# A top-1 expert layer: the routing of its first half issued in pieces between the blocks of its shared expert

## The chip, the core and the metric

The kernel runs on one core of a Trainium2 chip. A core has five engines, each with its own instruction queue, which it works through in order: TensorE (PE, matrix products and transposes; its weight loads are a row of their own, PEld), VectorE (DVE, elementwise work and reductions), ScalarE (ACT, activation functions and copies), GpSimd (POOL, elementwise work and the issue of indirect DMAs) and SyncE (SP, the issue of plain DMAs). They wait for each other through semaphores. The metric is the device time of one execution in microseconds; a median over several runs is given.

## What is computed

A decoder of four layers; each has a self attention, a cross attention and a feed-forward part, all with a residual. x is 32 x 128 tokens of 128 floats. The change lies in the feed-forward part of layer 2, a top-1 mixture of seven experts with a shared eighth one that every token passes. Cut to what matters:

```python
def _L2_ffn_ref(x, Wr, Wu, Wg, Wd, Wu_s, Wg_s, Wd_s):
    def _swiglu(x, wu, wg, wd):
        up = x @ wu
        g = x @ wg
        gate = jax.nn.sigmoid(g) * g
        return up * gate @ wd
    logits = x @ Wr
    probs = jax.nn.softmax(logits, axis=-1)
    topk_vals, topk_idx = jax.lax.top_k(probs, TOP_K)
    out = jnp.zeros_like(x)
    for i in range(TOP_K - 1):
        p = topk_vals[..., i:i + 1]
        ind = topk_idx[..., i]
        acc = jnp.zeros_like(x)
        for j in range(NUM_EXPERTS - 1):
            mask = (ind == j).astype(x.dtype)[..., None]
            acc = acc + _swiglu(x, Wu[j], Wg[j], Wd[j]) * mask
        out = out + ALPHA * p * acc
    out = out + _swiglu(x, Wu_s, Wg_s, Wd_s)
    return out

x = x + _L2_ffn_ref(_layernorm(x, axis=-1), L2_ffn_Wr, ...)
```

With TOP_K 2 the loop runs once, so each token goes to its best expert, unless that is number 7, which has no expert. DIM is 128, HID 512.

## The kernel before

x stays on the chip in eight groups `xg[0]` to `xg[7]` of 512 tokens (4 tiles of 128). Most tiles come from pools with a fixed number of slots that are reused in turn: `bmid` (5 slots of 128x512), `gmid` (10), `bbig` (4 of 128x2048), the small `s` tiles, and in PSUM `ps`, `two` and `acc` (two slots each). A tile whose slots are all in use waits for the release of one. A scheduler orders each engine's instructions by the order of the program and by when it reckons them ready. Between `follow(T, A, V)` (L243) and `follow()` the engines named keep the order of the program; POOL and SP are never held to it. In this layer `follow` isn't used before the change; in the attention ahead of it and in the layer behind it is.

The layer is `layer8` (L1509), called once for each half of the tokens (side 0 is groups 0 to 3, side 1 groups 4 to 7), and driven by `layer8_first` (L1783):

1. `ready(i)` normalizes group i into `xn_all` (`norm`, L336: bn_stats and bn_aggr on DVE, an addition and a power on POOL, the scaling of four tiles on DVE). `gate(i)` turns it over on PE, copies it on ACT to `xnTs[i]`, a `gmid` tile, and takes the logits into one `acc` tile.
2. `route()` (L1551): softmax over 8 logits of 16 tiles at once, one Exp on ACT and the rest on DVE. `first_k` (L418) ranks by comparing all pairs, on two `bbig` tiles of 128x1024. It leaves the selection `ssel` and the weight of the expert `ww2`.
3. `place()` (L1566): two products with triangular and full matrices of ones, a scan and small DVE operations give each token its row `pos` in a buffer `xs` in DRAM sorted by expert, and each tile of sorted rows the row `wrow` of its expert's weights. POOL clears one of the scratch tiles (`keep8`, L1574).
4. `ready2(i)` normalizes half two. `send(c)` (16 times, L1606) stores a tile of 128 normalized tokens to `xs` by an indirect DMA from POOL. `load(t)` (L1633) fetches the weights of sorted tile t, 768 KB, into one of four `units` slots, also an indirect DMA from POOL. `rows(t)` (L1639) reads sorted rows, a plain DMA on SP, which waits for all stores, and copies their row numbers on POOL.
5. `shared(i, c)` (L1612): one of 16 blocks of the shared expert, group i and quarter c of the hidden width. Two up products into a `two` tile, Silu on ACT, product by gate on DVE, down product into an `acc` tile. Each 128x512 float32 product is two matmul passes in the trace. After the fourth quarter `add_out` (L409) copies the sum (ACT and DVE by turns, `evac`), turns it over and adds it to x. The shared weights `U[8]` hold one of the four `units` slots until the last block.
6. `gate2`, `route2`, then the experts of half one: `up(t)` and `down(t)` for 14 tiles of 256 rows, with further loads and rows, `place2` after tile 0, the stores of half two two by two, then `collect`. Half two's experts and its shared expert are handed to the next layer as work between its own steps.

Of the kernel before, what the change touches and what calls it, by code (L numbers as in the profile page):

```python
# [15 lines left out]
ALU = mybir.AluOpType  # L16
# [8 lines left out]
J = 4  # L25
# [177 lines left out]
def program(ctx, tc, cols, x, ctxt, mask, drop, dfirst, dsmall, dwide, drows, dunits, dexperts, dconst, drel, dwq, out):  # L203
# [32 lines left out]
    def bmid(shape=(128, 512)):  # L236
        return mid.tile(list(shape), F32, tag="bmid", name="bmid", bufs=5)

    def small(*shape):
        n = int(np.prod(shape))  # L240
        return sm.tile([128, *shape], F32, tag=f"s{n}", name="s", bufs=4 if n < 128 else 2)
# [12 lines left out]
    def flat(t):  # L254
        return t.rearrange("p a b -> p (a b)")

    def bc(ap, axis, n):

        ap = ap.unsqueeze(axis)
        shape = list(ap.shape)  # L260
        shape[axis] = n
        return ap.to_broadcast(shape)
# [73 lines left out]
    def norm(src, o, by=None, by2=None):  # L336

        st, mv, rs = small(J, 6), small(J, 2), small(J)
        for j in range(J):
            V.bn_stats(st[:, j, :], src[:, j, :])  # L340
        for j in range(J):
            V.bn_aggr(mv[:, j, :], st[:, j, :])
        if by is not None:
            P.tensor_tensor(rs, mv[:, :, 1], by2, ALU.mult)
            P.tensor_scalar(rs, rs, EPS, None, ALU.add)
        else:
            P.tensor_scalar(rs, mv[:, :, 1], EPS, None, ALU.add)
        P.tensor_tensor(rs, rs, K["nhalf"], ALU.pow)
        if by is not None:
            P.tensor_tensor(rs, rs, by, ALU.mult)  # L350
        for j in range(J):
            V.tensor_scalar(o[:, j, :], src[:, j, :], mv[:, j, 0:1], rs[:, j : j + 1], ALU.subtract, ALU.mult)
# [53 lines left out]
    def add_x(i, p):  # L406
        V.tensor_tensor(xg[i], xg[i], p, ALU.add)
# [7 lines left out]
            T.transpose(p[:, j, :], o[:, j * 128 : (j + 1) * 128], ident)  # L415
        add_x(i, p)

    def first_k(v, e, k, sel=None, n=J):  # L418

        tile_of = bmid if n * e * e <= 512 else bbig  # L420
        gt, eq = tile_of((128, n, e, e)), tile_of((128, n, e, e))
        other, own = bc(v, 2, e), bc(v, 3, e)
        V.tensor_tensor(gt, other, own, ALU.is_gt)
        V.tensor_tensor(eq, other, own, ALU.is_equal)
        tri = bc(K[f"tri{e}"], 1, n).rearrange("p a (i j) -> p a i j", i=e)
        V.tensor_tensor(eq, eq, tri, ALU.mult)
        V.tensor_tensor(gt, gt, eq, ALU.add)
        rank = small(n, e)
        sel = small(n, e) if sel is None else sel
        V.tensor_reduce(rank, gt, AX.X, ALU.add)  # L430
        V.tensor_scalar(sel, rank, k - 0.5, None, ALU.is_lt)
        return sel

    def parts3(w, parts):
# [1074 lines left out]
    def layer8(side):  # L1509
# [26 lines left out]
        ssel = sm.tile([128, N * J, 8], F32, tag="ssel", name="ssel", bufs=2)  # L1536
        ww2, pos = (sm.tile([128, N * J], dtype, tag=name, name=name, bufs=2) for name, dtype in (("ww2", F32), ("pos", I32)))
        wrow = sm.tile([128, TILES], I32, tag="wrow", name="wrow", bufs=2)
        xnTs, sums, ins, mids = {}, {}, {}, {}

        def ready(i):
            norm(xg[side * N + i], xn_all[:, i, :, 0:D])

        def gate(i):
            xnTs[i] = transposed(xn_all[:, i, :, 0:D], gmid(), A.copy)
# [5 lines left out]
        def route():  # L1551
            lg = sums.pop("l")
            l, m = bmid((128, N * J, 8)), small(N * J)
            V.tensor_reduce(m, lg, AX.X, ALU.max)
            V.tensor_tensor(l, lg, bc(m, 2, 8), ALU.subtract)
            A.activation(l, l, AF.Exp)
            V.tensor_reduce(m, l, AX.X, ALU.add)
            V.reciprocal(m, m)
            V.tensor_tensor(l, l, bc(m, 2, 8), ALU.mult)
            first_k(l, 8, 1, ssel, N * J)  # L1560
            V.tensor_scalar(l, l, 2.0, None, ALU.mult)
            V.tensor_tensor(l, ssel, l, ALU.mult)

            V.tensor_reduce(ww2, l[:, :, 0:7], AX.X, ALU.add)

        def place():  # L1566
            flat_sel = ssel.rearrange("p c e -> p (c e)")
            p = ps((128, 2, N * J * 8))
            mm(p[:, 0], K["upper"], flat_sel)
            mm(p[:, 1], K["ones"], flat_sel)  # L1570

            tot, ends, keep8 = (bmid((128, 8, N * J)) for _ in range(3))
            V.tensor_copy(tot, p[:, 1].rearrange("p (c e) -> p e c", e=8))
            P.memset(keep8, 1.0)  # L1574
            P.memset(keep8[:, :, 0:1], 0.0)
            V.tensor_tensor_scan(flat(ends), flat(keep8), flat(tot), 0.0, ALU.mult, ALU.add)
            rnd = 1.5 * 2.0**23

            nt, bt = small(8), small(8)
            V.tensor_scalar(nt, ends[:, :, N * J - 1], TOKENS / 2 - 0.5, 1.0 / TOKENS, ALU.add, ALU.mult)  # L1580
            V.tensor_scalar(nt, nt, rnd, rnd, ALU.add, ALU.subtract)
            below = small(8, 8)
            V.tensor_tensor(below, bc(nt, 1, 8), K["tri8"].rearrange("p (i j) -> p i j", i=8), ALU.mult)
            V.tensor_reduce(bt, below, AX.X, ALU.add)

            V.tensor_tensor(ends, ends, tot, ALU.subtract)
            first = small(8)
            V.tensor_scalar(first, bt, float(TOKENS), -1.0, ALU.mult, ALU.add)
            V.memset(first[:, 7:8], TILES * TOKENS - 1.0)
            V.tensor_tensor(ends, ends, bc(first, 2, N * J), ALU.add)  # L1590
            spot = bmid((128, N * J, 8))
            V.tensor_tensor(spot, p[:, 0].rearrange("p (c e) -> p c e", e=8), ends.rearrange("p e c -> p c e"), ALU.add)
            V.tensor_tensor(spot, spot, ssel, ALU.mult)
            posf = small(N * J)
            V.tensor_reduce(posf, spot, AX.X, ALU.add)
            V.tensor_copy(pos, posf)

            V.tensor_tensor(bt, bt, nt, ALU.add)
            past = bmid((128, TILES, 7))
            V.tensor_tensor(past, bc(K["count"][:, 0:TILES], 2, 7), bc(bt[:, 0:7], 1, TILES), ALU.is_ge)  # L1600
            ef = small(TILES)
            V.tensor_reduce(ef, past, AX.X, ALU.add)
            V.tensor_scalar(ef, ef, 6.0, 128.0, ALU.min, ALU.mult)
            V.tensor_tensor(wrow, ef, K["row"].to_broadcast([128, TILES]), ALU.add)

        def send(c):  # L1606
            at = bass.IndirectOffsetOnAxis(ap=pos[:, c : c + 1], axis=0)
# [1 line left out]
            tc.add_to_no_dep_group(f"rows{side}", d.ins)  # L1609
            tc.declare_no_dep(d.ins, group=f"rows{side}", reason="every token has a row of its own")  # L1610

        def shared(i, c):  # L1612
            if c == 0:
                sums[i] = acc()
            w8 = U[8]
            block = slice(c * 128, (c + 1) * 128)
            pa = two()
            mm(pa[:, 0], w8[:, 0:512][:, block], xnTs[i])
            mm(pa[:, 1], w8[:, 512:1024][:, block], xnTs[i])
            h = bmid()  # L1620
            A.activation(h, pa[:, 1], AF.Silu)
            V.tensor_tensor(h, h, pa[:, 0], ALU.mult)
            mm(sums[i], w8[:, 1024:1536][:, block], h, c == 0, c == 3)
            if c == 3:
                add_out(side * N + i, sums.pop(i))
                xnTs.pop(i)
                if i == N - 1:
                    U.pop(8)


        half = TOKENS // 128
# [143 lines left out]
            for i in range(N):  # L1775
                yield lambda: None, lambda i=i: collect(i)

        return ready, gate, route, place, send, shared, load, rows, up, down, collect, TILES, pieces


    beside = []
# [1 line left out]
    def layer8_first():  # L1783
        N = G // 2
        ready, gate, route, place, send, shared, load, rows, up, down, collect, TILES, _ = layer8(0)
        ready2, gate2, route2, place2, send2, _, load2, rows2, *_, pieces = layer8(1)
        for i in range(N):
            ready(i)
            gate(i)
        route()  # L1790
        place()
        for i in range(N):
            ready2(i)
        for c in range(N * J):
            send(c)
        load(0)
        load(1)
        load(2)
        rows(0)
        rows(1)  # L1800
        for i in range(N):
            for c in range(4):
                shared(i, c)
        for i in range(N):
            gate2(i)
        route2()
        later = [lambda c=c: send2(c) for c in range(N * J)]
        up(0)
        for t in range(TILES):
            if t + 3 < TILES:  # L1810
                load(t + 3)
            if t + 2 < TILES:
                rows(t + 2)
            if t + 1 < TILES:
                up(t + 1)
            down(t)
            if t == 0:
                place2()
            for _ in range(2 if t > 1 else 0):
                if later:  # L1820
                    later.pop(0)()
        for i in range(N):
            collect(i)

        def start():
            load2(0)
            load2(1)
            load2(2)
            rows2(0)
            rows2(1)  # L1830

        beside.append(start)
        beside.extend(pieces())
# [324 lines left out]
```

## Time and profile before

Most instructions carry the line of a helper (L192), so groups and stages are told apart by tiles and by time.

| | |
|---|---|
| runs shown, median (lowest to highest) | 2979.89 us (2970.95 to 2987.02) |
| profiled execution, its own time | 2967.81 us |
| its span, first to last instruction | 2965.9 us |
| PE, DVE, ACT, POOL busy | 86%, 70%, 51%, 33% |
| mean granted TensorE clock | 0.917 |
| chain that ended last, shares | PE 52%, DVE 29%, ACT 7%, POOL 7%, issue 3%, DMA 2% |

Busy shares are means over twelve parts with different limits; the layer of the change takes from about 2256 to 2447 us. A row of the timeline gives start, duration, engine, line, operation, the tiles written and read, and in brackets how long the engine had been idle and what released it. Durations are those of one execution.

The marks of the layer in the trace: the last matmul of half one's logits ends at 2267.8; `pos` and `wrow` are written at 2282.1 and 2282.2; the 16 stores are issued from 2282.6 to 2306.8; the shared expert's last down product ends at 2334.8; the logits of half two end at 2343.2; the experts' products run from 2343.5 to about 2435.8; half one's rows are collected at 2451.

### The profile page before, as it was taken

To read this page: it belongs to the slowest core of one execution; us is meant where nothing else is said; L and a number is where in the kernel's file an instruction comes from. 1 tells how busy PE (TensorE), PEld (TensorE's weight loads), DVE (VectorE), ACT (ScalarE), POOL (GpSimd) and SP (SyncE) were. 2 spreads that over 40 slices of the span, in tenths; PEclk is the share of its full clock that TensorE was granted. 3 is DMA by queue.
4 is the path that set the end of the run, shared out by engine and by line. 5 is a ranking of instruction groups with operands and counts; after the bars stand their busy time and mean duration, and the time that the engine had idled before them with its cause. 6 is when DMAs were issued, how large, how long until landed. Compare 5 with 4: busy or idle time off the path is not lost.

```text
span 2965.9 us, 55573 instructions
## 1 busy us (share of the span) xinstructions
PE 2552.0 (86%) x22609; PEld 1641.3 (55%) x22628; DVE 2072.2 (70%) x4121; ACT 1504.4 (51%) x3360; POOL 972.2 (33%) x1009
## 2 busy tenths in 40 slices
PE   6889999999889989999998999987886977976664
PEld 3555667777644446566664444445554666644443
DVE  6877667878878756677786544458886415789893
ACT  4555545444412256666664444457773323456663
POOL 4443342223210123334551000124442365324432
PEclk8877789999999999999999999989997998998786
DMA  3000000000000010000000000000002255210000
GB/s 113 2 2 2 6 20 8 5 8 1 12 11 1 0 33 2 5 9 9 12 2 15 1 1 0 1 1 2 2 2 82 94 179 166 91 29 12 22 11 18
DMA packets 50464, 73.44 MB, mean 25 GB/s; under 512 B 3841, under 2 KB 40962, under 8 KB 50082
## 3 DMA queue, kind: packets, MB, share of 16 engines
q1 hardware_dynamic: 41968, 33.05, 3.7%
q0 software_dynamic: 7808, 33.71, 3.5%
q8 instruction: 178, 2.92, 0.4%
q10 hardware_dynamic: 434, 3.14, 0.3%
q14 instruction: 76, 0.62, 0.1%
HBM read 57.00 MB, written 12.89 MB: 24 GB/s over the span
## 4 chain that ended last, share of the span: by engine, by line
PE 52%; DVE 29%; ACT 7%; POOL 7%; issue 3%; DMA 2%; DVEq 0%; ACTq 0%; POOLq 0%; SPq 0%
PE ps L192 21%; PE two L192 17%; PE acc L192 14%; DVE bbig L192 12%; DVE s L192 9%; DVE bmid L192 3%; DVE gmid L192 3%; ACT bbig L192 3%; POOL xn L399 3%; ACT bmid L192 1%; ACT xn L192 1%; POOL s L397 1%; DVE x L192 1%; ACT gmid L192 1%; DMA we<-in_experts,wrow 1%
## 5 line engine op out<-in xcount | busy, mean ns | idle before, releaser
L192 PE MATMUL ps<-cs,bbig 128*128 128x128 f32 x2208 | 330.3, 290 | 83.4 <-ACT bbig L192 34.6
L192 PEld LDWEIGHTS ps<-cs,bbig 128*128 128x128 f32 x2208 | 254.8, 147 | 187.3 <-ACT bbig L192 84.0
L192 ACT COPY bbig<-ps 128x512 f32<-128x512 f32 x418 | 229.2, 591 | 241.5 <-PE ps L192 241.4
L192 DVE TENSOR_REDUCE s<-two 128x8 f32<-128x1024 f32 (+1 forms) x192 | 234.1, 1220 | 119.6 <-PE two L192 118.4
L192 PE MATMUL two<-xnT,u 128*128 128x512 f32 x512 | 262.4, 613 | 11.8 <-ACT bmid L192 6.3
L192 DVE TENSOR_TENSOR bbig<-bbig 128x1024 f32<-128x1024 f32 (+3 forms) x234 | 249.6, 1108 | 7.3 <-ACT bbig L192 5.8
L192 PE MATMUL acc<-bmid,u 128*128 128x512 f32 x416 | 221.3, 619 | 20.1 <-DVE bmid L192 18.8
L192 PE MATMUL two<-gbig,gmid 32*128 32x512 f32 (+1 forms) x1248 | 216.5, 567 | 2.4 <-ACT bbig L192 2.4
L192 DVE TENSOR_TENSOR bmid<-bmid,ps 128x512 f32<-128x512 f32 x192 | 130.0, 684 | 114.8 <-ACT bmid L192 94.7
L479 POOL TENSOR_SCALAR gbig<-bmid,cs 128x512 f32<-128x512 f32 x96 | 148.7, 1565 | 162.8 <-ACT bmid L192 162.8
L192 ACT ACTIVATE bbig<-two,s 128x256 f32<-128x256 f32 (+1 forms) x512 | 189.7, 419 | 20.8 <-DVE s L192 17.4
L192 ACT ACTIVATE bbig<-bbig 128x512 f32<-128x512 f32 (+1 forms) x160 | 128.1, 801 | 87.1 <-DVE bbig L192 86.6
L192 PEld LDWEIGHTS two<-xnT,u 128*128 128x128 f32 x512 | 92.8, 193 | 116.4 <-issue 56.5
L192 ACT ACTIVATE bmid<-two 128x512 f32<-128x512 f32 x88 | 52.5, 597 | 183.3 <-PE two L192 175.0
L192 ACT ACTIVATE bmid<-two,ws 128x512 f32<-128x512 f32 x128 | 85.1, 686 | 115.1 <-PE two L192 115.0
L192 PEld LDWEIGHTS acc<-bmid,u 128*128 128x128 f32 x416 | 76.7, 197 | 115.1 <-DVE bmid L192 60.8
L192 ACT ACTIVATE bbig<-bbig,s 128x128 f32<-128x128 f32 x384 | 118.7, 388 | 29.0 <-DVE s L192 29.0
L1068 POOL TENSOR_TENSOR bbig<-bbig,s 128x1024 f32<-128x1024 f32 x32 | 60.6, 1893 | 214.2 <-PE two L192 152.7
L192 DVE TENSOR_TENSOR bbig<-two,s 128x1024 f32<-128x1024 f32 (+1 forms) x128 | 122.6, 958 | 9.0 <-ACT bbig L192 0.5
L491 POOL MEMSET val<- 128x512 f32 x72 | 39.5, 551 | 259.1 <-PE acc L192 258.1
L192 PE MATMUL ps<-cs,xn 128*128 128x128 f32 x288 | 66.5, 320 | 65.3 <-ACT xn L192 36.9
L192 PE MATMUL two<-xT,we 128*128 128x128 f32 (+1 forms) x576 | 102.5, 333 | 18.8 <-DMA we<-in_experts,wrow 14.8
(313 smaller groups left out, 5914.2 us busy)
## 6 DMA issues: line engine op xcount, KB each, us to landing
u<-in_units SPq DMA_DIRECT2D x10, 768.0 KB, 4.3
gmid<-in_ctx SPq DMA_DIRECT2D x16, 256.0 KB, 3.0
x<-in_x SPq DMA_DIRECT2D x8, 256.0 KB, 9.1
gmid<-in_mask SPq DMA_DIRECT2D x8, 256.0 KB, 3.1
ys<-bbig SPq DMA_DIRECT2D x2, 1024.0 KB, 6.6
gmid<-ys SPq DMA_DIRECT2D x8, 256.0 KB, 4.0
gmid<-in_drop SPq DMA_DIRECT2D x8, 256.0 KB, 3.4
out<-x SPq DMA_DIRECT2D x8, 256.0 KB, 2.4
```

The source lines that it names most:

```text
L192: d = f(*args, **kwargs)
L397: P.tensor_tensor(rs, rs, K["nhalf"], ALU.pow)
L399: P.tensor_scalar(xn[:, j, :], xg[i][:, j, :], mv[:, j, 0:1], rs[:, j : j + 1], ALU.subtract, ALU.mult)
L479: P.tensor_scalar(o[:, n, :], k, K["n4"][:, n : n + 1], None, ALU.mult)
L491: P.memset(o, 0.0)
L1068: (V if c2 else P).tensor_tensor(pr[:, four, :], pr[:, four, :], bc(nm[:, four], 2, 256), ALU.mult)
```

## The change

The routing functions become generators that give control back at marked places (`yield`), and the shared block is cut into four functions. After the logits of half one, all that follows runs as rounds under `follow(T, A, V)`: in round k the up products and Silu of block k, two pieces of routing, where it is due the turn-over and addition of the group that ended two rounds before, the down product of block k-1, and the gate product of block k. There are 21 pieces: the norm sums of half two (4), `route` (8), `place` (5), then, in one go with the first scaling of half two's norm, the three weight fetches, the 16 stores and the two row reads, and the other scalings. Thus the norm's sums and power are issued ahead of routing and its scalings behind the stores, and the fetches ahead of the stores. Scratch tiles of `place` come from `gmid` in place of `bmid`; the addition of EPS in half two's norm moves from POOL to DVE; the shared sums are all copied by ACT. Half two's `route2` and `place2` run the same pieces without a break between them.

```diff
+    def first_k_steps(v, e, k, sel, n):
...
         V.tensor_tensor(gt, other, own, ALU.is_gt)
+        yield
         V.tensor_tensor(eq, other, own, ALU.is_equal)
+        yield
...
         V.tensor_tensor(eq, eq, tri, ALU.mult)
+        yield
         V.tensor_tensor(gt, gt, eq, ALU.add)
         rank = small(n, e)
-        sel = small(n, e) if sel is None else sel
+        yield
         V.tensor_reduce(rank, gt, AX.X, ALU.add)
         V.tensor_scalar(sel, rank, k - 0.5, None, ALU.is_lt)
+        yield
...
+        def ready_first(i):
+            if i == 0:
+                norms.update(mv=small(N, J, 2), rs=small(N, J))
+            x, st, mv, rs = xg[side * N + i], small(J, 6), norms["mv"][:, i], norms["rs"][:, i]
+            for j in range(J):
+                V.bn_stats(st[:, j, :], x[:, j, :])
+            for j in range(J):
+                V.bn_aggr(mv[:, j, :], st[:, j, :])
+            V.tensor_scalar(rs, mv[:, :, 1], EPS, None, ALU.add)
+            P.tensor_tensor(rs, rs, K["nhalf"], ALU.pow)
+
+        def ready_second(i):
+            x, mv, rs = xg[side * N + i], norms["mv"][:, i], norms["rs"][:, i]
+            for j in range(J):
+                V.tensor_scalar(xn_all[:, i, j, 0:D], x[:, j, :], mv[:, j, 0:1], rs[:, j : j + 1], ALU.subtract, ALU.mult)
...
             A.activation(l, l, AF.Exp)
+            yield
...
-            first_k(l, 8, 1, ssel, N * J)
+            yield
+            yield from first_k_steps(l, 8, 1, ssel, N * J)
...
-            tot, ends, keep8 = (bmid((128, 8, N * J)) for _ in range(3))
+            tot, ends, keep8 = (gmid((128, 8, N * J)) for _ in range(3))
...
-        def shared(i, c):
+        def shared_up(i, c):
+            block = slice(c * 128, (c + 1) * 128)
+            pa = two()
+            mm(pa[:, 0], U[8][:, 0:512][:, block], xnTs[i])
+            mm(pa[:, 1], U[8][:, 512:1024][:, block], xnTs[i])
+            blocks[i, c] = pa, bmid()
+            A.activation(blocks[i, c][1], pa[:, 1], AF.Silu)
+
+        def shared_gate(i, c):
+            pa, h = blocks[i, c]
+            V.tensor_tensor(h, h, pa[:, 0], ALU.mult)
+
+        def shared_down(i, c):
+            _, h = blocks.pop((i, c))
             if c == 0:
                 sums[i] = acc()
...
+            mm(sums[i], U[8][:, 1024:1536][:, c * 128 : (c + 1) * 128], h, c == 0, c == 3)
             if c == 3:
-                add_out(side * N + i, sums.pop(i))
                 xnTs.pop(i)
+                o = sums["o"] = bmid()
+                A.copy(o, sums.pop(i))
...
+        def shared_add(i):
+            o, p = sums.pop("o"), ps((128, J, 128))
+            for j in range(J):
+                T.transpose(p[:, j, :], o[:, j * 128 : (j + 1) * 128], ident)
+            add_x(side * N + i, p)
...
-        route()
-        place()
-        for i in range(N):
-            ready2(i)
-        for c in range(N * J):
-            send(c)
-        load(0)
-        load(1)
-        load(2)
-        rows(0)
-        rows(1)
-        for i in range(N):
-            for c in range(4):
-                shared(i, c)
+
+        def pieces_of_routing():
+            for i in range(N):
+                ready2[1](i)
+                yield
+            yield from route()
+            yield from place()
+            load(0)
+            load(1)
+            load(2)
+            for c in range(N * J):
+                send(c)
+            rows(0)
+            rows(1)
+            for i in range(N):
+                ready2[2](i)
+                yield
+
+        routing = pieces_of_routing()
+        blocks = [(i, c) for i in range(N) for c in range(4)]
+        follow(T, A, V)
+        for k in range(len(blocks) + 2):
+            if k < len(blocks):
+                shared_up(*blocks[k])
+            for _ in range(2):
+                next(routing, None)
+            if k > 1 and blocks[k - 2][1] == 3:
+                shared_add(blocks[k - 2][0])
+            if k and k <= len(blocks):
+                shared_down(*blocks[k - 1])
+            if k < len(blocks):
+                shared_gate(*blocks[k])
+        for _ in routing:
+            pass
+        follow()
```

More of the change, by code (lines that the diff above doesn't have):

```diff
@@ L416, in add_out @@
         add_x(i, p)
-    def first_k(v, e, k, sel=None, n=J):
+    def first_k_steps(v, e, k, sel, n):
         tile_of = bmid if n * e * e <= 512 else bbig
@@ L423, in first_k @@
         V.tensor_tensor(gt, other, own, ALU.is_gt)
+        yield
         V.tensor_tensor(eq, other, own, ALU.is_equal)
+        yield
         tri = bc(K[f"tri{e}"], 1, n).rearrange("p a (i j) -> p a i j", i=e)
         V.tensor_tensor(eq, eq, tri, ALU.mult)
+        yield
         V.tensor_tensor(gt, gt, eq, ALU.add)
         rank = small(n, e)
-        sel = small(n, e) if sel is None else sel
+        yield
         V.tensor_reduce(rank, gt, AX.X, ALU.add)
         V.tensor_scalar(sel, rank, k - 0.5, None, ALU.is_lt)
+        yield
+    def first_k(v, e, k, sel=None, n=J):
+        sel = small(n, e) if sel is None else sel
+        for _ in first_k_steps(v, e, k, sel, n):
+            pass
         return sel
@@ L1538, in layer8 @@
         wrow = sm.tile([128, TILES], I32, tag="wrow", name="wrow", bufs=2)
-        xnTs, sums, ins, mids = {}, {}, {}, {}
+        xnTs, sums, ins, mids, norms, blocks = {}, {}, {}, {}, {}, {}
         def ready(i):
             norm(xg[side * N + i], xn_all[:, i, :, 0:D])
+        def ready_first(i):
[12 more added lines that the diff above has]
+                V.tensor_scalar(xn_all[:, i, j, 0:D], x[:, j, :], mv[:, j, 0:1], rs[:, j : j + 1], ALU.subtract, ALU.mult)
         def gate(i):
@@ L1584, in place @@
             V.tensor_reduce(bt, below, AX.X, ALU.add)
+            yield
             V.tensor_tensor(ends, ends, tot, ALU.subtract)
@@ L1590, in place @@
             V.tensor_tensor(ends, ends, bc(first, 2, N * J), ALU.add)
-            spot = bmid((128, N * J, 8))
+            spot = gmid((128, N * J, 8))
             V.tensor_tensor(spot, p[:, 0].rearrange("p (c e) -> p c e", e=8), ends.rearrange("p e c -> p c e"), ALU.add)
             V.tensor_tensor(spot, spot, ssel, ALU.mult)
+            yield
             posf = small(N * J)
@@ L1596, in place @@
             V.tensor_copy(pos, posf)
+            yield
             V.tensor_tensor(bt, bt, nt, ALU.add)
-            past = bmid((128, TILES, 7))
+            past = gmid((128, TILES, 7))
             V.tensor_tensor(past, bc(K["count"][:, 0:TILES], 2, 7), bc(bt[:, 0:7], 1, TILES), ALU.is_ge)
@@ L1604, in place @@
             V.tensor_tensor(wrow, ef, K["row"].to_broadcast([128, TILES]), ALU.add)
+            yield
         def send(c):
@@ L1610, in send @@
             tc.declare_no_dep(d.ins, group=f"rows{side}", reason="every token has a row of its own")
-        def shared(i, c):
+        def shared_up(i, c):
[10 more added lines that the diff above has]
+            _, h = blocks.pop((i, c))
             if c == 0:
                 sums[i] = acc()
[L1615 to L1623, printed above, removed]
+            mm(sums[i], U[8][:, 1024:1536][:, c * 128 : (c + 1) * 128], h, c == 0, c == 3)
             if c == 3:
-                add_out(side * N + i, sums.pop(i))
                 xnTs.pop(i)
+                o = sums["o"] = bmid()
+                A.copy(o, sums.pop(i))
                 if i == N - 1:
                     U.pop(8)
+        def shared_add(i):
[3 more added lines that the diff above has]
+            add_x(side * N + i, p)
         half = TOKENS // 128
@@ L1776, in pieces @@
                 yield lambda: None, lambda i=i: collect(i)
-        return ready, gate, route, place, send, shared, load, rows, up, down, collect, TILES, pieces
+        shared = shared_up, shared_gate, shared_down, shared_add
+        return (ready, ready_first, ready_second), gate, route, place, send, shared, load, rows, up, down, collect, TILES, pieces
     beside = []
@@ L1786, in layer8_first @@
         ready2, gate2, route2, place2, send2, _, load2, rows2, *_, pieces = layer8(1)
+        shared_up, shared_gate, shared_down, shared_add = shared
         for i in range(N):
-            ready(i)
+            ready[0](i)
             gate(i)
-        route()
-        place()
-        for i in range(N):
-            ready2(i)
-        for c in range(N * J):
-            send(c)
-        load(0)
-        load(1)
-        load(2)
-        rows(0)
-        rows(1)
-        for i in range(N):
-            for c in range(4):
-                shared(i, c)
+        def pieces_of_routing():
+            for i in range(N):
+                ready2[1](i)
+                yield
+            yield from route()
[9 more added lines that the diff above has]
+                ready2[2](i)
+                yield
+        routing = pieces_of_routing()
[13 more added lines that the diff above has]
+        for _ in routing:
+            pass
+        follow()
         for i in range(N):
             gate2(i)
-        route2()
+        for _ in route2():
+            pass
         later = [lambda c=c: send2(c) for c in range(N * J)]
@@ L1817, in layer8_first @@
             if t == 0:
-                place2()
+                for _ in place2():
+                    pass
             for _ in range(2 if t > 1 else 0):
```

## The prediction, made before the change was run

> **What bounds the kernel now.** The page first: TensorE (PE) is busy 86% of the span and holds 52% of the chain that ended last, VectorE (DVE) 29%. The chain says where this layer lies in it: after the attention's tail it runs through routing (DVE) from 2268 us, through the stores on GpSimd (POOL) and their waits from 2280 to 2293, and from 2294 on through PE: the shared expert, the logits of half two, the experts. So I read the layer by stage, in windows. Columns are PE, its weight loads, DVE, ScalarE (ACT), POOL, each busy us, then PE's granted clock:
>
> ```profile
> 2256.00:2268.00 12.00, 11.33 (x127) 9.14 (x120) 8.78 (x30) 2.25 (x4) 3.15 (x4) 0.98 0.63 214
> 2268.00:2284.50 16.50, 1.96 (x6) 0.93 (x4) 14.23 (x54) 2.79 (x4) 3.02 (x4) 0.57 0.08 31
> 2284.50:2297.40 12.90, 6.54 (x8) 2.38 (x9) 3.86 (x13) 0.00 (x0) 11.04 (x14) 0.50 0.11 37
> 2297.40:2335.50 38.10, 36.80 (x94) 15.55 (x92) 12.80 (x19) 9.53 (x16) 11.35 (x16) 1.00 0.28 90
> 2335.50:2343.50 8.00, 7.38 (x57) 6.89 (x57) 0.96 (x2) 3.88 (x6) 0.50 (x1) 0.90 0.34 114
> ```
>
> Rows two and three are 29.4 us in which PE works 8.5, half of that at half clock. Row four is the shared expert, PE-bound at full clock; row five the logits of half two, after which the experts' matmuls begin (2343.5). The timeline of PE shows the hole:
>
> ```profile
> 2267.67 1.10 PE L192 MATMUL two<-gmid,u 128*128 128x512 f32 x2
> 2276.39 1.19 PE L192 MATMUL ps<-ssel,cs 128*128 128x128 f32 x4 [7.61 <-DVE ssel L192]
> 2284.50 2.08 PE L192 MATMUL acc<-bmid,u 128*128 128x512 f32 x2 [6.92 <-DVE bmid L192]
> 2286.37 1.91 PE L192 MATMUL two<-gmid,u 128*128 128x512 f32 x2
> 2294.64 2.07 PE L192 MATMUL acc<-bmid,u 128*128 128x512 f32 x2 [6.36 <-DVE bmid L192]
> 2296.51 3.22 PE L192 MATMUL two<-gmid,u 128*128 128x512 f32 x6
> 2299.57 1.02 PE L192 MATMUL acc<-bmid,u 128*128 128x512 f32 x2
> ```
>
> Two shared blocks have their up products by 2268.7 (both `two` buffers full), then PE waits for DVE. On DVE the first gate product stands behind all of routing, the second behind half two's norm, which waits for POOL:
>
> ```profile
> 2283.79 0.66 DVE L192 TENSOR_TENSOR bmid<-bmid,two 128x512 f32<-128x512 f32 x1
> 2289.17 2.15 DVE L192 TENSOR_SCALAR bbig<-x,s 128x128 f32<-128x128 f32 x8 [4.72 <-POOL s L348]
> 2292.88 1.28 DVE L192 TENSOR_SCALAR bbig<-x,s 128x128 f32<-128x128 f32 x4 [1.56 <-POOL s L348]
> 2293.91 0.68 DVE L192 TENSOR_TENSOR bmid<-bmid,two 128x512 f32<-128x512 f32 x1
> ```
>
> On POOL the powers of that norm (1.06 us each) stand among the 16 stores; after the stores come three weight fetches, then the wait for the first rows:
>
> ```profile
> 2305.80 0.96 POOL L1608 DMA_INDIRECT xs<-bbig,pos  x1 [0.31 <-issue]
> 2307.07 1.00 POOL L1635 DMA_INDIRECT we<-in_experts,wrow  x1 [0.30 <-issue]
> 2308.37 0.97 POOL L1635 DMA_INDIRECT we<-in_experts,wrow  x1 [0.30 <-issue]
> 2309.65 0.94 POOL L1635 DMA_INDIRECT we<-in_experts,wrow  x1 [0.30 <-issue]
> 2317.83 0.18 POOL L1643 COPY at<-xt 128x2 int32<-128x2 int32 x1 [7.25 <-DMA xt<-xs]
> ```
>
> Rows are there at 2317.8, PE comes for them at 2341: today they have 23 us of slack.
>
> **What the change makes of it.** Two paths now lead to the experts' first matmul. I work out each.
>
> DVE's order is written out: in round k two pieces of routing, an addition to x in each fourth, then gate product k (0.62 us apart when back to back). PE per round: four up passes and two down passes at 0.43 us each, 2.58 us (a row of 2 takes 1.02 with its drain; in the steady stretch four blocks and a turn take 10.87 us). DVE by rows, start to start, from 2263.8 where it now finishes half one's norm:
> - Rounds 0 and 1: norm sums of two groups each: 8 bn_stats at 0.22, 8 aggregates at 0.08, two 4-element operations at 0.1, the gate: 3.1 us each. To 2270.0; the logits are there at 2267.85, so routing starts 2.2 us later than today.
> - Round 2: softmax, 2.0 us today from 2267.85 to 2269.84, with the gate 2.6. The Exp stands behind Silu of blocks 0 to 2, so two table loads are new (1.28 us by the row at 2268.89); one lies before Exp. Silu 2 ends about 2270.4, the load about 2271.7, Exp was due 2271.05: 0.65 late. The Trainium skill (ScalarE: Activation LUTs, What ACT_TABLE_LOAD costs) adds a drain of 1.38 us to each switch, which would make it 2.0 late; the trace shows Exp ending 2268.87 and the load beginning 0.02 later, so I take 0.65. To 2273.3.
> - Rounds 3 and 4: two 128x1024 operations (1.2 each) and a gate: 3.0 each. Round 5: reduce, selection, weights 2.2, addition 0.69, gate 0.62: 3.5. Round 6: 1.8 with gate 2.5. Round 7: 1.75 and gate, 2.4. Round 8: 0.95 to the weight rows.
> Sum: 2273.3+3.0+3.0+3.5+2.5+2.4+0.95 = weight rows at 2288.7 against 2282.4 today, 6 us later; that delay is the price of the six gates and the norm sums put before it.
>
> POOL path: three fetches of 1.28 and 16 stores of 1.265 from 2288.9: last store issued at 2313.0. The powers are out of the queue (4.3 us less), the fetches moved in front (3.8 more): nil. Today the rows' transfer is issued 2.27 us after the last store's end and then takes 8.8 us beside three 768 KB fetches; now those were fetched 20 us before, and a row transfer has its median of 2.5: rows at 2317.8, transposes and copy as now 1.5 us: experts' matmuls at 2319.5. Should stores come before fetches in POOL's queue after all, 3.8 less and 6.3 more: 2322.
>
> PE path: pace of DVE to round 8 (gate 8 at 2290.5 after the four scalings of half two, 0.27 each), round 9 3.5, round 10 1.7, then PE alone: 20 us from gate 8 to the last down product by count (down 8 to 15 6.9, up 10 to 15 10.3, two turns 1.3, waits 1.5): 2310.5; logits of half two 7.4 busy and waits, 8: 2318.5. The two paths end within a us of each other. ACT gets all four output copies (0.58 each, two were DVE's): ACT is busy 1 us in 4 there, hidden. Scratch moved from `bmid` to `gmid`: 4 inputs and 5 scratch tiles of 10, and it leaves `bmid` to the blocks. gt and eq stay in `bbig`, whose four slots are the two xn and these two.
>
> So the experts start at 2320 instead of 2343.5: **23 us**. Behind them nothing moves: half two's routing, its sends and the fourth fetch (released today at 2335, then at 2311 or after the rows) keep their distance to the experts, and layer 9 starts from the collected rows; so the whole rest shifts. One plus not counted: half two's scan waits 3.45 us for a POOL clear of a `bmid` tile; in `gmid` it may come sooner, 0 to 3 us.
>
> **The clock.** What could undo this is a rule of the Trainium skill (TensorE: Matmul & The Clock Gate, HAM clock gate and its second failure mode): PE runs at half clock until it was busy for a window of about 3.4 us, falls back after an idle one, and frequent short gaps between groups can make it swing. The trace's own rows:
>
> ```profile
> 2240.31 0.63 PE L192 MATMUL ps<-cs,bbig 128*128 128x128 f32 x4 [2.14 <-DVE x L192]
> 2250.34 1.97 PE L192 MATMUL ps<-cs,bbig 128*128 128x128 f32 x8 [2.67 <-ACT bbig L192]
> ```
>
> After 2.14 us idle 4 matmuls take 0.63 (full), after 2.67 8 take 1.97 against 1.14. The new gaps are a round minus 2.58: 0 to 0.9 us, about 1.5 in round 2. The nearest stretch is the attention before, 2130 to 2165: PE busy 28.4 of 35 us with gaps up to 1.4, clock 0.95. By the row the seven DVE-paced rounds lose about 1 us of PE; by the rule at its worst they run at half clock, 5.16 a round against 3: 15 us, and the gain is 8. I take the row.
>
> **Sum.** The profiled execution took 2967.8 (span 2965.9) and becomes 2945; the runs shown have median 2979.9, 12 above it, so the median becomes **2957**.
>
> **Rivals.**
> (a) Half clock through all blocks, the losing side: from 2268 14 ups of 3.44, 16 downs of 1.72, turns 4.4: to 2348; logits 10 instead of 8; experts at 2358, 15 later: **2995**. It decides once gaps reach 2.1 to 2.7 us a round, or if short gaps count. For it: clock 0.50 in the third window. Against: that window has idle times of 6 us. 12%.
> (b) Rounds slower than summed (gates waiting for Silu, a static order that puts logits behind a down product, swings of the clock as above): each us a round delays both paths 7; at 1.6 us a round the gain is 12: **2968**. For it: three engines in lockstep with two `two` buffers. Against: gate, down, up, Silu is a cycle of about 4.5 us per two rounds. 20%.
> (c) The change doesn't do what it says: pieces are placed, but the rest of the program, whose order isn't written out here, is rearranged and the layer's start waits elsewhere: **2980**, nothing gained. For: POOL is busy almost without a break from 2362 to 2405 and PE waits 6 us for a fetch there. Against: that stretch starts from half two's routing, which shifts too. 7%.
> Forecast: 61%, 2951 to 2963.
>
> **Numbers.** A measurement here tells about 0.5% (15 us) from no change. Faster by over 0.5% (below 2965): nearly all of the forecast, a third of (b): 0.67. Slower by over 0.5%: half of (a) and a little for the unforeseen: 0.11. Between: 0.22. The range 2945 to 2979 leaves out (a), most of (c) and a tenth of luck beyond the low end (scan earlier, clock better).
>
> **What would show it.** PE busy above 75% from 2268 to 2311 with clock above 0.85; weight rows about 2288 to 2290; stores 16 in a row with no power among them, after three fetches; experts' first products near 2320; from there to the end the same 622 us as now (2343.5 to 2965.9). Wrong: clock near 0.5 in the rounds (a), rounds over 4 us (b), or a shorter front and a longer rest (c).

## The result and the profile after

| | before | after |
|---|---|---|
| median of 13 runs each (lowest to highest) | 2981.46 us (2967.62 to 2988.73) | 2958.59 us (2948.28 to 2980.76) |
| ratio after to before, 95% interval | | 0.9932 [0.9912, 0.9952] |
| profiled execution, its span | 2967.81, 2965.9 us | 2958.57, 2956.8 us |
| mean granted TensorE clock | 0.917 | 0.925 |

The change gains about 20 us, and about 15 in a second comparison of the same two kernels (e1 below); the forecast was 23.

The two profiled executions are not aligned: the attention ahead of the layer, which the change doesn't touch, ends 14 us earlier in the trace of after. So I count from the attention's last product, which begins at 2257.7 before and at 2243.7 after. The windows of after, by the same stages as before (PE, its weight loads, DVE, ACT, POOL busy, then PE's granted clock, DMA share, GB/s):

```profile
2249.00:2261.50 12.50, 12.50 (x47) 8.31 (x46) 5.41 (x28) 4.03 (x6) 1.90 (x2) 0.64 0.52 169
2261.50:2282.50 21.00, 19.61 (x50) 8.65 (x51) 16.55 (x41) 7.64 (x11) 1.62 (x4) 1.00 0.00 1
2282.50:2301.00 18.50, 18.49 (x49) 8.11 (x47) 9.22 (x25) 4.75 (x8) 14.14 (x15) 1.00 0.50 171
2301.00:2311.00 10.00, 3.22 (x5) 0.80 (x4) 1.36 (x2) 0.64 (x2) 3.92 (x8) 0.74 0.29 79
2311.00:2323.80 12.80, 12.21 (x57) 11.41 (x58) 0.98 (x2) 4.54 (x7) 0.99 (x1) 0.50 0.23 73
```

Rows two and three are routing and the stores. PE, which worked 8.5 of 29.4 us there, now works 38.1 of 39.5, at full clock. Rows four and five are new: a hole of 6.8 us at the end of the shared expert, and the logits of half two at half clock. In PE's timeline:

```profile
2264.00 1.88 PE L192 MATMUL two<-gmid,u 128*128 128x512 f32 x4
2267.21 1.12 PE L192 MATMUL acc<-bmid,u 128*128 128x512 f32 x2 [1.32 <-DVE bmid L192]
2268.17 1.88 PE L192 MATMUL two<-gmid,u 128*128 128x512 f32 x4
2270.08 1.12 PE L192 MATMUL acc<-bmid,u 128*128 128x512 f32 x2
...
2308.79 2.08 PE L192 MATMUL acc<-bmid,u 128*128 128x512 f32 x2 [5.93 <-DVE bmid L192]
2311.59 1.12 PE L192 MATMUL ps<-cs,bmid 128*128 128x128 f32 x4 [0.73 <-ACT bmid L192]
```

Up to 2301 the longest idle time of the rounds is 1.32 us, in the round of the Exp. The same round on DVE, and the end of routing:

```profile
2261.53 0.29 DVE L192 TENSOR_REDUCE s<-acc 128x16 f32<-128x128 f32 x1 [0.41 <-PE acc L192]
2261.85 0.29 DVE L192 TENSOR_TENSOR bmid<-acc,s 128x128 f32<-128x128 f32 x1
2265.66 0.29 DVE L192 TENSOR_REDUCE s<-bmid 128x16 f32<-128x128 f32 x1 [3.51 <-ACT bmid L192]
...
2282.29 0.17 DVE L192 TENSOR_TENSOR wrow<-s,cs 128x14 int32<-128x14 f32 x1
2282.38 1.21 DVE L192 TENSOR_SCALAR bbig<-x,s 128x128 f32<-128x128 f32 x4
2283.40 0.68 DVE L192 TENSOR_TENSOR bmid<-bmid,two 128x512 f32<-128x512 f32 x1
```

The scalings of half two's norm (2282.38) wait for nothing: the 4.72 and 1.56 us before are gone. POOL has its 16 stores without a power among them, though four of them slip in front of the fetches; the first rows are there 3.62 us after the last store:

```profile
2285.13 0.96 POOL L1641 DMA_INDIRECT xs<-bbig,pos  x1 [0.30 <-issue]
2286.39 0.99 POOL L1680 DMA_INDIRECT we<-in_experts,wrow  x1 [0.30 <-DVE bbig L192]
...
2304.14 0.96 POOL L1641 DMA_INDIRECT xs<-bbig,pos  x1 [0.30 <-issue]
2308.72 0.18 POOL L1688 COPY at<-xt 128x2 int32<-128x2 int32 x1 [3.62 <-DMA xt<-xs]
```

And what made the hole of 5.93 us, on ScalarE:

```profile
2295.47 0.60 ACT L192 ACTIVATE bmid<-two 128x512 f32<-128x512 f32 x1 [1.13 <-PE two L192]
2300.36 0.60 ACT L192 ACTIVATE bmid<-two 128x512 f32<-128x512 f32 x1 [4.29 <-remote]
2307.42 0.60 ACT L192 ACTIVATE bmid<-two 128x512 f32<-128x512 f32 x1 [6.46 <-remote]
```

Silu 14 and 15 start 1.9 and 6.4 us after their up products ended (2298.45, 2301.02); "remote" means that no record shows what released them. More such waits, up to 8.20 us, stand among the experts. The trace of before has none.

Marks from the attention's last product, in us (start of the weight rows' write, of the last matmul pass of the last down product, of the experts' first product):

| trace | weight rows | last down | experts |
|---|---|---|---|
| before | 24.5 | 76.4 | 85.8 |
| before, second trace (e5) | 24.5 | 79.6 | 88.9 |
| after | 38.6 | 66.1 | 80.1 |
| after, second trace (e1) | 34.7 | 62.0 | 76.0 |
| forecast for after | 31.0 | 51.8 | 62.3 |

So the traces show the experts 6 to 13 us earlier, less than the medians gained. Three questions: what closed the hole, the rounds or something beside them; do the standstills belong to the change; and where are the missing microseconds.

### The profile page after: what moved, and what is told of

Read it like the earlier page. It is cut to its first block, busy times and chain, and to the rows that moved or that the text cites. A ratio compares the mean times of both kernels' runs of the same rounds, so it can differ in the third digit from the quotient of the medians.

```text
span 2956.8 us, 55569 instructions
## 1 busy us (share of the span) xinstructions
PE 2538.6 (86%) x22609; PEld 1634.0 (55%) x22628; DVE 2072.5 (70%) x4123; ACT 1507.1 (51%) x3364; POOL 971.8 (33%) x1005
## 4 chain that ended last, share of the span: by engine, by line
PE 51%; DVE 30%; ACT 7%; POOL 6%; issue 3%; DMA 2%; another core or an unknown queue 1%; DVEq 0%; ACTq 0%; POOLq 0%; SPq 0%
PE ps L192 20%; PE two L192 17%; PE acc L192 14%; DVE bbig L192 11%; DVE s L192 9%; DVE bmid L192 4%; POOL xn L399 3%; DVE gmid L192 3%; ACT bbig L192 3%; ACT bmid L192 1%; ACT xn L192 1%; POOL s L397 1%; DVE x L192 1%; ACT gmid L192 1%
## 5 line engine op out<-in xcount | busy, mean ns | idle before, releaser
L192 PE MATMUL ps<-cs,bbig 128*128 128x128 f32 x2208 | 334.3, 292 | 83.3 <-ACT bbig L192 34.7
L192 DVE TENSOR_TENSOR h<-h,two 128x512 f32<-128x512 f32 x66 | 45.2, 686 | 108.8 <-ACT h L192 103.2
```

Of the source, the lines that this page charges most:

```text
L192: d = f(*args, **kwargs)
```

## The experiments

All ten were timed beside the kernel before, in three groups (e1 to e4, e5 to e8, e9 and e10); a ratio is to the runs of before in its own group. Marks are counted from the attention's last product, as in the table.

### The changed kernel again (no edit)

> The changed kernel once more, unaltered, for a second trace: in the first one ScalarE stands still between 2296 and 2307 us and again between 2349 and 2363 us on waits whose release the trace doesn't show, which cost about 10 and 14 us there. Theory A (these standstills belong to that one execution): the second trace has none of that size at these places, the shared expert ends about 24 us earlier than before the change and the experts' products start 20 to 24 us earlier, counted from the end of the attention; median 0.9925 +- 0.003 of before. Theory B (the change brings them about, since fetches and stores now run beside the blocks): they are there again at the same instructions, and the gain counted from the end of the attention is under 10 us.

Median 2962.44 us, ratio 0.9951 [0.9932, 0.9969]. In its trace the same two Silus stand still, 4.11 and 6.46 us, so they are not an accident of one execution. The profiled execution itself took 2979.58, the longest of this kernel's 18 in the group: a single trace is no measure of the time.

### Fetches behind the stores

```diff
+            for c in range(N * J):
+                send(c)
             load(0)
             load(1)
             load(2)
-            for c in range(N * J):
-                send(c)
```

> The changed kernel with the three weight fetches behind the 16 stores again. Theory (fetch order is worth little): the stores end 3.8 us earlier, the first rows take up to 9 us instead of 2.5 to land beside the fetches, so the experts start 0 to 3 us later than in the changed kernel; ratio to before within 0.002 of the changed kernel's. Rival (fetches ahead carry the gain): ratio 0.997 or higher.

Ratio 0.9955 [0.9932, 0.9978], experts at +76.7, against 0.9951 and +76.0 in e1: no difference. The fetches ahead of the stores bring nothing that can be measured.

### No rounds: all pieces of routing first, then the blocks, without the written order

```diff
-        follow(T, A, V)
+        for _ in routing:
+            pass
```

> The changed kernel without its rounds: all routing pieces first, then the shared blocks, order left to the scheduler; the norm split and the fetches ahead stay. Theory (the rounds carry most of it): the hole of about 16 us on TensorE between the second block's up products and the first gate product is back, the second hole of 8 us is not; the experts start 6 to 10 us earlier than before the change, ratio 0.997 +- 0.002. Rival (norm sums and fetches ahead of the stores carry it): ratio 0.993 as with the whole change.

Ratio 0.9956 [0.9937, 0.9976], experts at +74.9. The hole doesn't come back. The scheduler itself puts gate products between routing's operations; DVE's timeline of this kernel:

```profile
2270.19 1.22 DVE L192 TENSOR_TENSOR bbig<-bmid 128x1024 f32<-128x1024 f32 x1
2271.34 0.68 DVE L192 TENSOR_TENSOR bmid<-bmid,two 128x512 f32<-128x512 f32 x1
2271.93 1.22 DVE L192 TENSOR_TENSOR bbig<-bmid 128x1024 f32<-128x1024 f32 x1
```

So something else in the change lets it do so. Left over are the scratch tiles in `gmid` and the split norm.

### Rounds with half two's norm left whole, behind routing; fetches behind the stores

```diff
-            for i in range(N):
-                ready2[1](i)
-                yield
             yield from route()
             yield from place()
+            for i in range(N):
+                ready2[0](i)
+                yield
+            for c in range(N * J):
+                send(c)
             load(0)
             load(1)
             load(2)
-            for c in range(N * J):
-                send(c)
             rows(0)
             rows(1)
-            for i in range(N):
-                ready2[2](i)
-                yield
```

> The rounds alone: half two's norm whole and behind place, stores before fetches, as before the change. Theory (the split of the norm is what lets the rounds work): on GpSimd the powers stand between the stores, one even behind the wait for the first rows, and on VectorE, now held to the program's order, the gate products of rounds 6 and later stand behind the scalings that wait for them; the blocks stop several times and end after the first rows have landed, about 2320 us and later; experts at 2345 to 2352, ratio 1.000 to 1.003. Rival (the rounds suffice): ratio 0.993 to 0.995.

Ratio 1.0022 [1.0003, 1.0042], median 2988.07, experts at +103.1. With the order of the program held, every gate product behind a scaling waits with it for POOL, where the powers stand among the stores. DVE and PE of this kernel:

```profile
2298.24 1.27 DVE L192 TENSOR_SCALAR bbig<-x,s 128x128 f32<-128x128 f32 x4 [8.46 <-POOL s L348]
2299.27 0.68 DVE L192 TENSOR_TENSOR bmid<-bmid,two 128x512 f32<-128x512 f32 x1
...
2308.43 1.28 DVE L192 TENSOR_SCALAR bbig<-x,s 128x128 f32<-128x128 f32 x4 [7.42 <-POOL s L348]
```

```profile
2300.00 2.07 PE L192 MATMUL acc<-bmid,u 128*128 128x512 f32 x2 [9.46 <-DVE bmid L192]
2315.34 2.08 PE L192 MATMUL acc<-bmid,u 128*128 128x512 f32 x2 [9.86 <-DVE bmid L192]
```

An order written out turns one late operand into a standstill of everything behind it. The split norm is what the rounds need.

### Before, a second trace (no edit)

> The kernel before, unchanged, for a second trace. Waits of ScalarE whose release no record shows stand in the trace of the changed kernel (4.3 to 8.2 us each) and in those of its four variants, and in none of the one trace of before. Theory A (they come of the change: the fetches and stores now stand close together): none here either, experts' first products 85 to 87 us after the attention's last product, their last 178 us. Theory B (they come of the taking of the profile, whatever the kernel): some of 4 us or more here too, in the stretch of stores and experts, and the experts' end 3 to 5 us later than in the first trace. The time is 2975 and the ratio 1.000 by both.

Ratio to itself 0.9991 [0.9971, 1.0011]: that is how well such a comparison closes. The standstills are here too. ACT and then PE of this trace:

```profile
2297.17 0.60 ACT L192 ACTIVATE bmid<-two 128x512 f32<-128x512 f32 x1 [4.43 <-remote]
2369.98 0.60 ACT L192 ACTIVATE h<-two 128x512 f32<-128x512 f32 x1 [6.40 <-remote]
```

```profile
2371.35 0.80 PE L192 MATMUL acc<-we,h 128*128 128x128 f32 x2 [5.78 <-issue]
```

So they are not peculiar to the change. What sets the first trace of before apart is its records: it holds 3707 of DMA landings, this second one of the same program 2826, and 701 of the 881 missing lie between 2250 and 2490 us, this layer. The page's list of DMA issues shows it (the last number is the time to landing), first trace, then second:

```profile
u<-in_units SPq DMA_DIRECT2D x10, 768.0 KB, 4.3
```

```profile
u<-in_units SPq DMA_DIRECT2D x10, 768.0 KB
```

The trace of after and those of the nine experiments that keep all stores lack 870 to 1050 of these records, and all have standstills. The Trainium skill (NOTIFIC — the notification-queue block, 7.1 Overflow) says that records can be dropped when their queue is full, and that the block's inner pipeline holds back the engines that write them. The traces fit this, without proving it: the standstills come in the stretches of the stores and of the experts, where most of the missing records fall. That the taking of records is the cause was not tried by itself, and a rival, that the stores' traffic holds ScalarE up in every execution, can't be told from it by the traces.

### Scratch in gmid alone, in the kernel before

```diff
-            tot, ends, keep8 = (bmid((128, 8, N * J)) for _ in range(3))
+            tot, ends, keep8 = (gmid((128, 8, N * J)) for _ in range(3))
...
-            spot = bmid((128, N * J, 8))
+            spot = gmid((128, N * J, 8))
...
-            past = bmid((128, TILES, 7))
+            past = gmid((128, TILES, 7))
```

> Before, with place's five scratch tiles in gmid and nothing else. Theory (two separate holes: the first is a lack of free bmid slots, which keeps the gate products behind routing; the second is half two's norm with its powers among the stores): the first hole goes, gate products 0 to 4 stand among routing's operations, the second stays: DVE waits 4 to 5 us for a power in the stores; experts' first products at +76 to +80 after the attention, ratio 0.996 to 0.998. Rival 1 (slots are all of it): experts at +75, ratio 0.9945 as in the run without rounds. Rival 2 (the norm is all of it): nothing gained, 1.000.

Ratio 0.9964 [0.9944, 0.9984], experts at +75.3. Five tiles taken from another pool close the first hole. DVE of this kernel:

```profile
2277.34 0.68 DVE L192 TENSOR_TENSOR bmid<-bmid,two 128x512 f32<-128x512 f32 x1
2278.44 0.69 DVE L192 TENSOR_TENSOR bmid<-bmid,two 128x512 f32<-128x512 f32 x1 [0.42 <-ACT bmid L192]
2279.04 1.22 DVE L192 TENSOR_TENSOR bbig<-bmid 128x1024 f32<-128x1024 f32 x1
...
2298.79 2.15 DVE L192 TENSOR_SCALAR bbig<-x,s 128x128 f32<-128x128 f32 x8 [4.72 <-POOL s L348]
```

Gate products now stand among routing's operations; the 4.72 us for the power, the second hole, is as it was, and PE waits 7.30 us there. In its trace no standstill falls into the shared blocks.

### The split norm alone, in the kernel before

```diff
+        for i in range(N):
+            ready2[1](i)
         route()
         place()
-        for i in range(N):
-            ready2(i)
         for c in range(N * J):
             send(c)
+        for i in range(N):
+            ready2[2](i)
```

> Before, with half two's norm sums and powers ahead of routing, and scratch in bmid as before. Theory (two separate holes): the gate products still come after the weight rows, and those come later by the 16 sums and scalings of DVE ahead of them, 4 to 7 us; then no wait for a power: experts' first products at +79 to +83, ratio 0.996 to 0.999. Rival 1 (slots are all of it): 1.000 or slower. Rival 2 (the norm is all of it): experts at +75, ratio 0.9945.

Ratio 0.9985 [0.9968, 1.0002], experts at +84.8, where +79 to +83 was expected: too little to be told from nothing. No wait for a power is left, but the gate products still stand behind the weight rows, and PE waits as before:

```profile
2279.32 1.20 PE L192 MATMUL ps<-ssel,cs 128*128 128x128 f32 x4 [10.09 <-DVE ssel L192]
2285.09 3.78 PE L192 MATMUL acc<-bmid,u 128*128 128x512 f32 x4 [4.58 <-DVE bmid L192]
```

### Both, in the kernel before

The edits of the last two together; no rounds, fetches behind the stores.

> Before, with both: scratch in gmid and the norm's sums and powers ahead of routing. No rounds, blocks of the shared expert as before, weight fetches behind the stores. Theory: the whole gain of the change, ratio 0.993 to 0.996, experts' first products at +75 to +77, DVE's order of gate products the scheduler's own. Rival (rounds or fetches ahead are needed for a part of it): 0.997 or above.

Ratio 0.9947 [0.9924, 0.9969], median 2963.42, experts at +77.0, with one standstill of 6.45 us in the shared blocks. It is the whole gain of the change as far as these intervals can tell, and the parts, 0.36% and 0.15%, add up to about its 0.53%, though the second alone can't be told from nothing. The cutting into pieces, the written order and the moved fetches aren't needed.

### The changed kernel with the scratch in bmid

The edit of the scratch tiles the other way round.

> The changed kernel with place's five scratch tiles in bmid again; the order of DVE, ScalarE and PE is held by the rounds and stays. Theory (slots decided only because the scheduler puts the gate products behind routing when bmid is full; an order held by the program does the same without free slots): routing's tiles and the blocks share five slots, some Silus of rounds 5 to 8 wait 1 to 2 us for one; ratio 0.994 to 0.997, experts' first products at +77 to +83 after the attention's last product. Rival (the slots themselves carry the gain, with rounds too): Silu waits for place's tiles, weight rows later by 5 us or more, experts at +85 or later, ratio 0.998 to 1.002.

Ratio 0.9959 [0.9942, 0.9976], experts at +73.1, earlier than expected, weight rows at +33.2. So the slots decide only as long as the scheduler may choose: when `bmid` is full it puts the gate products behind routing; with the order held they stay where they are, and five slots are enough.

### The changed kernel without half one's stores

```diff
-            for c in range(N * J):
-                send(c)
```

> The changed kernel without half one's 16 stores of normalized tokens: the experts of half one work on the buffer's first contents, with all their products, fetches and stores as before. For the standstills of ScalarE at Silu 14 and 15 (4.3 and 6.5 us in two traces of the changed kernel). Theory (they come of DMA traffic, the 16 stores beside the three weight fetches): both are gone, the last down product at +55 to +59 after the attention in place of +62 to +66, experts' first products at +63 to +68, full clock in the logits of half two. Rival (they belong to the place in the program, whatever the DMAs do): both still at Silu 14 and 15, experts at +75 to +80. The time says little of it: ratio 0.988 to 0.995.

Both standstills of the shared blocks are gone; routing, the rest of the shared blocks, and the logits of half two:

```profile
2267.70:2288.50 20.80, 19.41 (x50) 8.60 (x50) 16.38 (x41) 7.52 (x11) 0.84 (x7) 1.00 0.00 1
2288.50:2310.00 21.50, 20.63 (x53) 8.79 (x51) 10.67 (x27) 5.70 (x11) 3.25 (x4) 1.00 0.34 110
2310.00:2319.70 9.70, 8.70 (x57) 8.21 (x58) 0.98 (x2) 4.27 (x7) 0.89 (x1) 0.77 0.31 97
```

Last down product at +59.2, experts at +69.8, 10 us earlier than in the trace of after, though up to 2 us later than expected, and the logits of half two have a clock of 0.77, not the full one expected. Among the experts, where half two is still stored, the waits without a releaser remain (6.38 us at one Silu). Yet the ratio is 0.9941 [0.9918, 0.9964], no better than with the stores. Ten microseconds that are there in the trace and not in the times: this again speaks for standstills that come with the taking of the trace. It isn't proof, since the interval holds some 7 us to either side.

## Why the prediction came out, step by step

**What bounds the kernel: right.** Two holes, one before the weight rows and one at the powers, are separate: each goes with its own edit (e6, e7). That their gains add is likely but weakly shown, since the interval of e7 includes no gain.

**What closes the first hole: right for this kernel, but not the reason given.** The prediction gave it to DVE's written order and noted of the scratch tiles only that they leave `bmid` to the blocks. Either is enough by itself: the slots without the order (e6, e3), the order without the slots (e9). The row that told of it stands in the trace of before, on ACT:

```profile
2278.47 1.26 ACT L192 ACTIVATE bmid<-two 128x512 f32<-128x512 f32 x2 [8.29 <-DVE bmid L192]
```

Two Silus wait 8.29 us, and what releases them is not PE, whose products were long there, but DVE's last use of a `bmid` tile.

**The rounds: mis-sized by 2 us.** From the start of routing to the weight rows 18.7 were summed, 20.8 measured. The excess is the Exp: it was reckoned 0.65 us late and DVE waits 3.51 for it, against 0.43 before. About 0.3 of this is a slip in the sum: by the rows of before the Exp is due 0.71 us after routing starts, at 2270.7, and 2271.05 is when it would be over. The table load takes 1.28 us as in the row taken (2264.02, 0.01 after Silu 2 ends, and the Exp at 2265.31), without the drain that the Trainium skill (ScalarE: Activation LUTs, What ACT_TABLE_LOAD costs) adds; what was missed is that Silu 2 itself starts only at 2263.41, since its up products stand behind the last logits on PE.

**The start of routing: right at full clock, 5.5 us late in the trace of after.** It was put at +12.3, by the norm sums and two gates on DVE ahead of it. In e1 and e9, where PE keeps full clock from the attention's last product to the last logits, DVE begins routing at +12.7 without waiting for the logits. In the traces of after and of e10 it begins at +17.8 and waits for them: PE falls to half clock at +4.0 and stays there for 10.2 us (hence the 0.64 in the first window above), though it had not been idle for more than 0.68 us at a time. In the trace of after:

```profile
2246.60 0.39 PE L192 MATMUL acc<-ws,gmid 128*128 128x8 f32 x2 [0.68 <-ACT gmid L192]
2247.24 0.49 PE L192 MATMUL ps<-ws,gmid 128*128 128x128 f32 x2 [0.26 <-DVE bbig L192]
...
2249.45 1.91 PE L192 MATMUL two<-gmid,u 128*128 128x512 f32 x2
```

The two passes of the last row take 1.02 us at full clock. ScalarE hands the delay on: Silu 0 with a table load waits 5.11 us for PE (load at 2255.39) and stands before the last two copies, for which the logits wait. In e2, e3 and e4 PE spends 3.4 to 6.8 us of this stretch at half clock and the last logits end at +14.1 to +15.0; in the five traces of before and e5 to e8 it keeps full clock there, and they end at +10.1 to +10.3. The prediction weighed swings of the clock for the rounds, and not for this stretch ahead of them.

**POOL's path: right.** From the weight rows to the last store's end 24.3 us forecast, 22.8 measured; the rows are there after 26.4 for 29.1. Moving the fetches was priced at nil and is nil (e2).

**PE's path: right where nothing stands still.** From the weight rows to the end of the last down product 21.8 us were summed; without the stores it is 21.3. In the trace of after it is 28.6, by the standstills, and the logits of half two take 12.9 us to the experts' first product in place of 9.5, at half clock.

These terms close the sum: 62.3 forecast, plus 5.5, plus 2.1, plus 6.8, plus 3.4 is 80.1, and the trace has 80.1. Without the standstills the trace of e10 has 69.8, which is 62.3 plus the first two terms and is 16 us before the 85.8 of before's trace without standstills. With routing at +12.7, as in e1 and e9, it would be 5 us less (an estimate from the two starts of routing). So the layer gains 16 to 21 us by the traces, and the medians gained 20 [14, 26] and 15 [9, 20] us. The forecast of 23 was too high by 2 to 7 us, all of it ahead of the weight rows. That the median came within 2 us of 2957 is in part luck: the two comparisons differ by more than that.

**The clock: right in the rounds, missed ahead of them.** The rounds run at 1.00 in the trace of after, with gaps of at most 1.32 us up to 2301; in e1 they lose the clock once, for 3.4 us from +12.4 on. The two rows from which the prediction read a limit between 2.14 and 2.67 us don't give one: in e5 eight matmuls after the same 2.67 us of idle time take 1.14 us, which is full clock, and in the trace of after the clock falls behind gaps of 0.68 us. Nor does the idle window of about 3.4 us of the Trainium skill (TensorE: Matmul & The Clock Gate, HAM clock gate) describe these traces: in the trace of before the granted clock falls at 2270.2, 1.4 us after PE's last matmul (1.00 from 2269 to 2270, 0.58 from 2270 to 2271, 0.50 after). The page's warning of swings by frequent short gaps (second failure mode) fits the start of the layer, and hardly the rounds. Why the same kernel keeps full clock there in e1 and loses it in the trace of after is open.

**The rest a pure shift: open.** From the experts' start to the end of the span the traces have 622.4 us (before), 636.1 (before again), 633.0 (after) and 635.3 (e1), where 622 was forecast; the same program differs by 14 from itself, so nothing smaller can be read there.

**The rivals.** Half clock through all blocks did not come, but the losing side was close by: the same rounds with the norm left whole lose about 0.2% (e4), by a mechanism that no rival named, the powers among the stores with a held order in front of them.

## What to carry to other kernels

Where an engine runs one long chain ahead of work that is ready, look first at the pool from which the waiting work takes its tiles: a scheduler that finds no free slot defers that work, and scratch moved to another pool did here what a hand-written order of 21 pieces did. Hold an order by hand only when every operand in it is early, since each late one then stops all that stands behind it. Take two traces of a kernel before you explain a wait in one, and believe the medians where the two disagree.

## What was not expected of the hardware

- Two traces of the same program differ by 15 us in where the layer starts and by 14 us from the experts to the end, with a total within 2 us (spans 2965.9 and 2967.8).
- In every trace with 2584 to 2835 DMA landing records ScalarE shows waits of 4 to 8 us with no recorded releaser, and in the one with 3707 none; Silu 14 and 15 of the changed kernel start 1.9 and 6.4 us after their products had ended. 16 stores less took these two away.
- PE fell to half clock for 10.2 us behind gaps of at most 0.68 us, in the trace of after and in e10, and kept full clock at the same place of the same kernel in e1.
- POOL's stores were issued every 1.26 us whether or not fetches of 768 KB were under way beside them, and the order of the two made no difference to the time.
